# Graph attention over a sparse adjacency: eight largest columns of each row taken with the degree, before the sort, instead of lists made after it

## Chip, cores and metric

One core of one Trainium2 chip. The time is the device time of one execution in microseconds (us); the median of several executions is given, and one further execution was recorded by the hardware profiler.

## The reference

Sixteen graphs of 1024 nodes with 512 features share one 1024 x 1024 adjacency matrix of zeros and ones. One attention layer with 8 heads of 64 is followed by a residual and a layer norm without scale or shift:

```python
q = (x @ Wq + bq).reshape(b, n, H, HD)          # k, v in the same way
scores = jnp.einsum('bqhd,bkhd->bhqk', q, k) / jnp.sqrt(jnp.float32(HD))
scores = scores + (1.0 - adj)[None, None, :, :] * -1000000000.0
attn = jax.nn.softmax(scores, axis=-1)
out = jnp.einsum('bhqk,bkhd->bqhd', attn, v).reshape(b, n, d)
x = _layernorm(x + (out @ Wo + bo), axis=-1)
```

A one at (i, j) has the probability 0.0039 times w[i] w[j], with w falling along the nodes, so that a row has few ones, some rows none and the first rows many. A row without any attends to all nodes alike.

## The kernel before, in words

**Sparse attention by gathers.** The rows are sorted by degree and worked on in eight tiles of 128 sorted rows. A *block* is one neighbour of each of the 128 rows of a tile: the keys and values of those neighbours are gathered from memory (`gather`, L951), VectorE multiplies them with the queries and adds up the heads (`products` L987, `scores` L1000), ScalarE makes the exponentials (L1004) and weighs the values, and VectorE adds the blocks up. Each row's first neighbours are its *own* blocks, `OWN = (2, 1, 2, 3, 4, 5, 5, 7)` for the eight tiles. Only tiles 6 and 7 have rows with more; their further edges are packed into 1 and 5 blocks (`BLOCKS`), where a partition holds any edge of the tile, and TensorE adds these up by a matrix of zeros and ones (`sums`, L1040). This makes 34 blocks a graph (tile 1 needs no block, its rows have one neighbour) and 544 in all.

**Fronts and finish.** A graph's *fronts* are transposes of x (`transpose_x`) and the products q, k, v in pairs of tiles (`pair`, L651), k and v by a seven-product scheme for 2x2 blocks of matrices that needs the weight combinations T1 to T4 (L321 to L326) and the sums of inputs s1 to s4 (`combine`, L615). k and v go to `kv_rows` and q to `q_rows` in memory. A finished tile is multiplied with Wo, normalised and stored in the order of the original rows.

**Order of the work.** The program is written out by hand (`manual_schedule`): a loop over steps `n`, one for a block, from `-LEAD_IN` on. Each step issues block n's work in its stages, then as much TensorE work as its `share` allows: in the lead-in the constants `LEAD_SHARE` and `LISTS_SHARE`, from step 0 on what is left until a goal that the planner sets for the end of each graph. Preparations are generators that advance by one `yield` in each step (`prep`, `preps`). Each engine runs its instructions in the order issued; GpSimd's queue (POOL) issues the indirect gathers, SP's the plain transfers. Four PSUM banks (`fill_psum`) turn round among the products.

**Making the lists, before.** All of this happens once, in front of and within the first graph:

- `ranks` (L370): the adjacency tiles are loaded, ScalarE adds up their rows (L382), the key degree*1024+row is spread over all partitions by TensorE (L392), and VectorE finds each row's rank (L405). (row, degree) is scattered to `order` by rank (L399) and read back in sorted order, `ranked` (L416 to L419), which gives `asked_row`, the original row at each sorted place. From the ranks each column also gets a code, place*2048+column+1, spread by eight more products (L434) into `CODE_OF`.
- `edges(t)` (L467), for each of the eight tiles, from the steps `EDGES_FROM`: gather the tile's adjacency rows in sorted order (L471), multiply with the codes (L477), take the eight largest of each row (L496; tile 7 first in segments of 64, ten rounds), take the code apart into the original row for graph 0 (`key_row0`) and the sorted place for the later graphs (`key_row`) (`decode`, L460), and for tiles 6 and 7 distribute the further edges over the blocks (L528 to L581).
- `checks` (L446): every entry of the adjacency must be 0 or 1; GpSimd clears each tile after it (L454).
- `sort_residual` (L810), at the steps -16 to -4: the rows of x that the last 26 tiles need as a residual are gathered in sorted order and stored to `residual`, from where `load_y` (L815) reads them near the end.

Of the kernel before, what the change touches and what calls it, by code (L numbers as in the profile page):

```python
# [10 lines left out]
F32 = mybir.dt.float32  # L11
BF16 = mybir.dt.bfloat16
I32 = mybir.dt.int32
AF = mybir.ActivationFunctionType
# [19 lines left out]
CODE, ROUND = 2048.0, 12582912.0  # L34
# [7 lines left out]
SORTED_AT = range(-16, -3)  # L42
# [6 lines left out]
LEAD_IN = 34  # L49
SEGMENT = 64  # L50
EDGES_FROM = (-17, -16, -15, -13, -11, -8, -7, -18)
# [4 lines left out]
LEAD_SHARE = 3.45  # L56
LISTS_SHARE = 4.6
# [106 lines left out]
def kernel(  # L164
# [48 lines left out]
    own = [sum(OWN[:t]) for t in range(NT)]  # L213
# [20 lines left out]
    with ExitStack() as main:  # L234
# [16 lines left out]
        SPAN = max(BLOCKS) * P  # L251
# [17 lines left out]
        key_row, key_row0 = (one.tile([P, NB], I32, name=name) for name in ("key_row", "key_row0"))  # L269
        query_row, query_row0 = (one.tile([P, NS], I32, name=name) for name in ("query_row", "query_row0"))  # L270

        absent = one.tile([P, NB - NS], F32, name="absent")
# [6 lines left out]
        asked, ranked = (one.tile([P, NT, 2], F32, name=name) for name in ("asked", "ranked"))  # L279
        key, rank, moved = (one.tile([P, NT], F32, name=name) for name in ("key", "rank", "moved"))  # L280
        rank_row, asked_row = (one.tile([P, NT], I32, name=name) for name in ("rank_row", "asked_row"))
        ADJ, CODE_OF = [], []
# [4 lines left out]
        order = dram.tile([N, 2], F32, name="order")  # L287
# [12 lines left out]
        def loads():  # L300
# [11 lines left out]
            for _ in range(3):  # L312
                yield
# [8 lines left out]
            yield  # L322
            nc.vector.tensor_tensor(T2, B22, T1, op=OP.subtract)
            yield
# [35 lines left out]
        now, plan, rest, urgent, known, waiting = [0], {}, {}, [], [], []  # L360
# [8 lines left out]

        def ranks():  # L370
# [4 lines left out]
            first_order = small.tile([P, 2 * NT], F32, name="order_first", bufs=1)  # L375
            nc.gpsimd.memset(first_order, 0.0)
            nc.gpsimd.dma_start(order.rearrange("(p t) c -> p (t c)", p=P), first_order)
            nc.vector.tensor_copy(asked[:, :, 0], query)
            for _ in range(4):
                yield  # L380
            for t in range(NT):
                nc.scalar.activation(ADJ[t], ADJ[t], AF.Copy, accum_out=asked[:, t, 1:2])  # L382
                if t % 3 == 2:
                    yield

            nc.vector.scalar_tensor_tensor(key, asked[:, :, 1], float(N), query, op0=OP.mult, op1=OP.add)
            keys = work.tile([P, N], F32, tag="kv", name="keys", bufs=5)
# [39 lines left out]
            nc.vector.tensor_tensor(moved, rank, moved, op=OP.add)  # L427
            nc.vector.tensor_scalar(key, query, 1.0, None, op0=OP.add)
            nc.vector.scalar_tensor_tensor(key, moved, CODE, key, op0=OP.mult, op1=OP.add)
# [3 lines left out]
            for t in range(NT):  # L433
                nc.tensor.matmul(pk[t // 4][:, ts(t % 4, P)], keys[:, ts(t, P)], ident, start=True, stop=True)  # L434
# [867 lines left out]
```

## Time and profile before

| | |
|---|---|
| median of 3 runs | 1949.38 us (1948.74 to 1950.09) |
| the profiled execution | 1952.72 us, its span 1951.0 us |
| granted TensorE clock, mean | 0.99 |
| transfers | 551.28 MB, mean 283 GB/s |

The busy tenths of the span's forty equal slices (48.8 us each):

```profile
DVE  2799999899999999899998998989899988999894
ACT  3514978888798888888887888888888888989794
POOL 1664676777677676766767576767767675756684
PEclk9989999999999999999999999999999999999998
DMA  7688888888888887887988788898988888998993
```

PE is TensorE, DVE VectorE, ACT ScalarE, POOL GpSimd. A digit is a tenth of the slice, 9 is 90% or more. In a row of a table of stretches stand the stretch, its length, the busy us of PE, PE's weight loads, DVE, ACT and POOL with their numbers of instructions, TensorE's granted clock, the DMA share and GB/s. In a timeline stand the start, the length, the engine, the line of the program, the operation and its tiles, and in brackets the idle time before it and what ended it. A row of waits names who waited for whom, the sum, how often, and the longest. The instructions that load x the first time and the weights lie in the first 30 us; the first block's product (L998) starts at 153.0 us, and the first graph's blocks end at 296.8 us.

### The profile page before, as it was taken

What the parts mean: (1) busy time and instruction counts of PE and PEld (TensorE: products, weight loads), DVE (VectorE), ACT (ScalarE), POOL (GpSimd) and SP (SyncE); (2) the same over time, 40 slices, a digit from 0 to 9 for tenths busy, and PEclk for the clock granted to TensorE, in tenths of its full rate; (3) what the DMA queues carried; (4) which work ended last, traced back from release to release, by engine and by line L of the source; (5) the groups of instructions that cost most, each with busy time, mean ns of one, the idle gap of its engine ahead of it and who ended that gap; (6) DMA issues with size and microseconds to landing.
All of it is one profiled execution on the core that took longest, in us unless ns stands there. A gap on an engine that the chain in (4) does not pass through costs nothing. (4 is left out here: it accounts for less than half of the span.)

```text
span 1951.0 us, 25391 instructions
## 1 busy us (share of the span) xinstructions
PE 1871.4 (96%) x5275; PEld 903.7 (46%) x5275; DVE 1741.1 (89%) x3604; ACT 1550.1 (79%) x6074; POOL 1295.9 (66%) x1205
## 2 busy tenths in 40 slices
PE   8979999999999999999999999999999999899896
PEld 3434444444545454454544444444544544344443
DVE  2799999899999999899998998989899988999894
ACT  3514978888798888888887888888888888989794
POOL 1664676777677676766767576767767675756684
PEclk9989999999999999999999999999999999999998
DMA  7688888888888887887988788898988888998993
GB/s 264 189 297 286 261 295 270 293 282 298 291 270 311 284 287 268 305 294 254 310 275 307 256 300 278 276 310 258 320 277 293 271 280 296 328 316 266 349 301 137
DMA packets 186050, 551.28 MB, mean 283 GB/s; under 512 B 31295, under 2 KB 31323, under 8 KB 185886
## 3 DMA queue, kind: packets, MB, share of 16 engines
q0 software_dynamic: 120528, 398.76, 62.5%
q1 hardware_dynamic: 62464, 145.30, 20.0%
q10 hardware_dynamic: 2894, 5.52, 0.8%
q14 instruction: 120, 0.98, 0.2%
q8 instruction: 44, 0.72, 0.1%
HBM read 433.86 MB, written 140.30 MB: 294 GB/s over the span
## 5 line engine op out<-in xcount | busy, mean ns | idle before, releaser
L1022 ACT ACTIVATE pv<-kvg,pv 128x64 f32<-128x64 f32 x3544 | 893.1, 339 | 3.2 <-issue 1.9
L977 POOL DMA_INDIRECT kvg<-kv_rows,key_row x544 | 623.6, 1146 | 330.9 <-issue 101.2
L634 PE MATMUL po<-wo,oT 128*128 128x512 f32 x944 | 438.1, 596 | 2.0 <-DVE y L857 1.1
L634 PE MATMUL pq<-wq,xT 128*128 128x512 f32 x904 | 422.5, 598 | 1.7 <-DVE q L664 1.3
L1002 DVE TENSOR_REDUCE s<-qk 128x8 f32<-128x512 f32 x544 | 369.8, 680 | 7.6 <-ACT pv L1012 0.5
L998 DVE TENSOR_TENSOR qk<-qt,kvg 128x512 f32<-128x512 f32 x448 | 306.1, 683 | 10.5 <-DMA kvg<-kv_rows,key_row 10.1
L634 PEld LDWEIGHTS po<-wo,oT 128*128 128x128 f32 x944 | 176.9, 191 | 195.3 <-issue 184.3
L634 PEld LDWEIGHTS pq<-wq,xT 128*128 128x128 f32 x904 | 168.9, 192 | 197.6 <-issue 183.8
L751 PE MATMUL pp<-t,s 128*128 128x512 f32 x504 | 239.2, 597 | 8.4 <-DVE s L620 4.5
L751 PE MATMUL x<-b,xT 128*128 128x512 f32 x504 | 239.7, 598 | 0.0
L1038 DVE TENSOR_TENSOR pv<-pv,pv 128x520 f32<-128x520 f32 x336 | 232.8, 693 | 4.4 <-ACT pv L1022 2.7
L805 POOL DMA_INDIRECT x<-in_x_dram,asked_row x120 | 135.8, 1132 | 89.0 <-PE pxT L605 62.2
L1012 ACT ACTIVATE pv<-s,absent 128x8 f32<-128x8 f32 x448 | 130.4, 293 | 67.0 <-DVE s L1002 48.0
L883 POOL DMA_INDIRECT out_dram<-y,asked_row x128 | 148.5, 1160 | 36.0 <-issue 27.1
L644 ACT ACTIVATE sq_k<-kv 128x128 f32<-128x128 f32 x512 | 150.8, 300 | 20.6 <-DVE kv L774 13.6
L751 PEld LDWEIGHTS pp<-t,s 128*128 128x128 f32 x504 | 95.0, 191 | 121.9 <-issue 114.4
L751 PEld LDWEIGHTS x<-b,xT 128*128 128x128 f32 x504 | 96.1, 193 | 114.1 <-issue 110.0
L805 POOL DMA_INDIRECT y<-in_x_dram,asked_row x102 | 113.4, 1112 | 30.8 <-issue 29.0
L751 PE MATMUL z<-b,s 128*128 128x512 f32 x252 | 121.9, 607 | 11.0 <-DVE kv L779 9.8
L947 POOL DMA_INDIRECT qg<-q_rows,query_row x96 | 105.2, 1096 | 34.0 <-issue 25.4
L751 PE MATMUL pp<-t,xT 128*128 128x512 f32 x252 | 118.5, 593 | 0.4 <-DVE q L664 0.4
L751 PE MATMUL z<-t,s 128*128 128x512 f32 x252 | 118.6, 593 | 0.0
(221 smaller groups left out, 2602.8 us busy)
## 6 DMA issues: line engine op xcount, KB each, us to landing
kv_rows<-kv SPq DMA_DIRECT2D x128, 512.0 KB
q_rows<-q SPq DMA_DIRECT2D x113, 256.0 KB
qt<-q_rows SPq DMA_DIRECT2D x105, 256.0 KB
kvg<-kv_rows,key_row POOLq DMA_INDIRECT x544
residual<-y_sorted SPq DMA_DIRECT2D x26, 256.0 KB
y<-residual SPq DMA_DIRECT2D x26, 256.0 KB
adj<-in_adj_dram POOLq DMA_DIRECT2D x8, 512.0 KB
spill<-oT SPq DMA_DIRECT2D x10, 256.0 KB
```

Source lines behind the costliest of these rows:

```text
L634: nc.tensor.matmul(p, lhs(c), w[:, c, :], start=(c == 0), stop=(c == NPAIR - 1))
L644: nc.scalar.activation(sq, s[:, ts(h, P)], AF.Square, scale=scale, accum_out=sums[:, h:h + 1])
L751: nc.tensor.matmul(R[bank], l[:, ts(c, P)], right[:, c, :], start=(first and c == 0), stop=(c == 1), skip_group_check=True,)
L805: nc.gpsimd.indirect_dma_start(out=y, out_offset=None, in_=x_rows, in_offset=bass.IndirectOffsetOnAxis(ap=asked_row[:, t:t + 1], axis=0), ...
L883: nc.gpsimd.indirect_dma_start(out=out_rows[b, t], out_offset=bass.IndirectOffsetOnAxis(ap=asked_row[:, t:t + 1], axis=0), in_=y, in_offse ...
L947: nc.gpsimd.indirect_dma_start(out=q, out_offset=None, in_=q_rows[b % ROWS], in_offset=bass.IndirectOffsetOnAxis(ap=rows, axis=0))
L977: nc.gpsimd.indirect_dma_start(out=KG[n], out_offset=None, in_=kv_rows[b % ROWS], in_offset=bass.IndirectOffsetOnAxis(ap=keys_of(b)[:, g:g ...
L998: nc.vector.tensor_tensor(QK[n], q, KG[n][:, 0:D], op=OP.mult)
L1002: nc.vector.tensor_reduce(S[n], QK.pop(n).rearrange("p (h d) -> p h d", d=HD), axis=AX.X, op=OP.add)
L1012: nc.scalar.activation(PV[n][:, D:], S.pop(n), AF.Exp, bias=bias)
L1022: nc.scalar.activation(pv[:, ts(h, HD)], v[:, ds(D + h * HD, HD)], AF.Copy, scale=pv[:, D + h:D + h + 1])
L1038: nc.vector.tensor_tensor(PV[b, t], PV[b, t], pv, op=OP.add)
```

## The change

The columns are looked for earlier, in the original order of rows. Right after the adjacency tiles are there (`most`), VectorE multiplies each with the column numbers 1 to 1024 and takes the eight largest of each row (`TOP`). They are scattered together with row and degree, so that `order` and `ranked` have ten numbers a row instead of two. After the sort, the own keys of all eight tiles are made at once from `ranked`. Places are no longer coded: each column's place is stored once to `place_of` in memory, and small indirect gathers (`places`) fetch 128 of them for each own block and each further block, into `key_row`. `edges` stays for tiles 7 and 6 alone (`REST_FROM`) and works with columns, not codes. The code products, `decode`, the clearing of adjacency tiles and the matrix of edges of its own (`of`) go.

T1 to T4 and Wo's load come later in the lead-in, behind most of the column search. `sort_residual` goes; the late tiles of x are stored to `residual` when they have been transposed, and the next load of x comes two steps later there. The lead-in has 39 steps instead of 34, with less TensorE work in its last 13 (`START_SHARE` 2.0 where 4.6 stood in the last 15).

```diff
-SORTED_AT = range(-16, -3)
-LEAD_IN = 34
-EDGES_FROM = (-17, -16, -15, -13, -11, -8, -7, -18)
+LEAD_IN = 39
+FRONT_BY = -14
+TOP = 8
+ADJ_AT = {-36: (0,), -35: (1, 2), -34: (3, 4), -33: (5,), -32: (6, 7)}
+CHECKS_AT = -27
+BIAS_AT = -8
+REST_FROM = {7: -24, 6: -9}
+PLACES_FROM = -22
-LEAD_SHARE = 3.45
-LISTS_SHARE = 4.6
+LEAD_SHARE = 3.3
+START_SHARE = 2.0
...
-            for _ in range(3):
+            for _ in range(5):
                 yield
             load_w(W["o"], wo)
...
+        def most(t, scratch):
+            nc.scalar.activation(ADJ[t], ADJ[t], AF.Copy, accum_out=asked[:, t, 1:2])
+            nc.vector.tensor_tensor(scratch, ADJ[t], place, op=OP.mult)
+            nc.vector.max(out=asked[:, t, 2:], in_=scratch)
...
-            nc.vector.tensor_tensor(moved, rank, moved, op=OP.add)
-            nc.vector.tensor_scalar(key, query, 1.0, None, op0=OP.add)
-            nc.vector.scalar_tensor_tensor(key, moved, CODE, key, op0=OP.mult, op1=OP.add)
-            nc.vector.tensor_copy(keys.rearrange("p (t q) -> p t q", t=NT), key[:, :, None].to_broadcast([P, NT, P]))
-            yield
-            pk = [fill_psum(f"pcodes_{i}") for i in range(2)]
-            for t in range(NT):
-                nc.tensor.matmul(pk[t // 4][:, ts(t % 4, P)], keys[:, ts(t, P)], ident, start=True, stop=True)
...
+            nc.vector.tensor_tensor(place_row, rank, moved, op=OP.add)
+            nc.sync.dma_start(place_of[0:N, :].rearrange("(t p) o -> p (t o)", p=P), place_row)
...
+            nc.vector.tensor_scalar(off, ranked[:, :, 2:3], 0.0, N + 1.0, op0=OP.is_le, op1=OP.mult)
+            nc.vector.tensor_tensor(ranked[:, :, 2:3], ranked[:, :, 2:3], off, op=OP.add)
+            nc.vector.tensor_scalar(ranked[:, :, 2:], ranked[:, :, 2:], -1.0, None, op0=OP.add)
+            yield
+            for tiles, K in ((slice(0, short), SHORT_KEYS), *((slice(t, t + 1), OWN[t]) for t in range(short, NT))):
...
+        def places(columns, per_step):
+            for i, g in enumerate(columns):
+                nc.gpsimd.indirect_dma_start(
+                    out=key_row[:, g:g + 1], out_offset=None, in_=place_of,
+                    in_offset=bass.IndirectOffsetOnAxis(ap=key_row0[:, g:g + 1], axis=0), bounds_check=N, oob_is_err=False,
+                )
...
-            for i in range(2):
-                nc.vector.tensor_tensor(v[:, ts(i, HALF)], v[:, ts(i, HALF)], CODE_OF[i], op=OP.mult)
+            nc.vector.tensor_tensor(v, v, place, op=OP.mult)
...
-            rows, high, missing = kr[:, 0, 0:K], kr[:, 1, 0:K], absent[:, own[t]:own[t] + K]
...
-            decode(rows, high)
...
-                    load_x(n // NT, n % NT)
+                    if b * NT + t >= SPILL[0]:
+                        nc.sync.dma_start(residual[b * NT + t - SPILL[0]], xs)
+                        later(2, lambda: load_x(n // NT, n % NT))
+                    else:
+                        load_x(n // NT, n % NT)
...
-        for t in range(NT):
-            prep.setdefault(EDGES_FROM[t], []).append(edges(t))
-        prep.setdefault(12 - LEAD_IN, []).append(bias_setup())
-        prep.setdefault(-22, []).append(checks())
+        for t, n in REST_FROM.items():
+            prep.setdefault(n, []).append(edges(t))
+        prep.setdefault(BIAS_AT, []).append(bias_setup())
+        prep.setdefault(CHECKS_AT, []).append(checks())
+        prep.setdefault(PLACES_FROM, []).append(places([NS + own[t] + i for t in range(NT) for i in range(OWN[t])], 3))
...
-                    share = LISTS_SHARE if n > -16 else LEAD_SHARE if n > -LEAD_IN else TRANSPOSE * 1.5
+                    share = START_SHARE if n > FRONT_BY else LEAD_SHARE if n > -LEAD_IN else TRANSPOSE * 1.5
...
-                if n in SORTED_AT:
-                    for i in range(2):
-                        sort_residual(2 * (n - SORTED_AT[0]) + i)
```

## The prediction

> **What bounds the kernel now.** I read the page's busy shares first, then the table of stretches (busy us of each engine), then what TensorE waited for in the first 200 us, then the timelines of TensorE and VectorE there.
>
> ```profile
> PE 1871.4 (96%) x5275; PEld 903.7 (46%) x5275; DVE 1741.1 (89%) x3604; ACT 1550.1 (79%) x6074; POOL 1295.9 (66%) x1205
> ```
> ```profile
> 0.00:22.10 22.10, 13.55 (x36) 6.71 (x36) 1.20 (x3) 3.53 (x5) 7.67 (x24) 1.00 0.92 344
> 22.10:48.90 26.80, 26.28 (x73) 12.83 (x74) 13.09 (x23) 14.91 (x40) 0.43 (x1) 0.94 0.53 197
> 75.00:123.90 48.90, 44.36 (x104) 19.41 (x103) 38.06 (x118) 15.53 (x49) 27.94 (x28) 0.93 0.87 298
> 123.90:150.30 26.40, 20.11 (x49) 8.21 (x49) 24.12 (x82) 5.37 (x21) 16.71 (x16) 0.94 0.85 300
> 150.30:297.00 146.70, 140.19 (x409) 68.25 (x408) 137.17 (x306) 108.81 (x456) 88.13 (x81) 1.00 0.83 280
> ```
> ```profile
> PE pxT L605 <- DMA x<-in_x_dram: 6.8, 2, 3.7
> PE pp L751 <- DVE s L620: 4.5, 1, 4.5
> PE z L751 <- DVE kv L779: 4.1, 1, 4.1
> PE pcodes L434 <- DVE keys L430: 2.5, 1, 2.5
> PE pk L723 <- DMA b<-in_L_gnn_Wk_dram: 2.3, 1, 2.3
> PE pp L751 <- DVE s L618: 1.7, 1, 1.7
> ```
> ```profile
> 38.06 1.88 PE L751 MATMUL pp<-t,s 128*128 128x512 f32 x4
> ...
> 112.21 3.75 PE L751 MATMUL pp<-t,s 128*128 128x512 f32 x4 [4.54 <-DVE s L620]
> 115.75 4.74 PE L634 MATMUL pq<-wq,xT 128*128 128x512 f32 x8
> ```
> ```profile
> 28.46 1.22 DVE L325 TENSOR_TENSOR t<-b,b 128x1024 f32<-128x1024 f32 x1
> ...
> 88.04 1.41 DVE L692 TENSOR_TENSOR vsum<-vsum,kv 128x512 f32<-128x512 f32 x2
> ...
> 99.98 1.21 DVE L496 MAX8 kl<-codes 128x8 f32<-128x1024 f32 x1
> ```
>
> TensorE bounds the whole: 1871 of 1951 us. From 297 to 1440 us it is busy 1132.89 of 1143. So only its losses count, and those that the change can touch lie at the front. Batch 0's list of blocks ends at 297 us (L1075's first reduction, at 296.8). Up to there TensorE is busy 268.1 us (the rows above and 23.62 from 48.9 to 75) and idle 28.9. Of that, 6.8 and 2.3 are first loads. The other 19.8 lie behind VectorE, nearly all between 105 and 180 us, where VectorE is busy 24.12 of 26.4 with the lists of all eight tiles. The clock falls with these waits: after the one of 4.54 us a group that takes 1.88 takes 3.75, one of 3.60 takes 4.74; such rows (pp, pq, pxT, z, x between 112 and 140) come to 5.2 us too much.
>
> **What the Trainium skill says.** "TensorE: Matmul & The Clock Gate", What's actually happening: an idle window of some 3.4 us halves the array's clock. The trace agrees: slow groups after 4.54 and 4.14 us, none after 2.48 (pcodes, 2.05 us against 1.95 for pkeys). "GPSIMD Engine Reference", Specifications: GpSimd shares its SBUF interface with VectorE in some modes. The trace fits: an 8-element VectorE operation took 2.29 us at 60.21 while GpSimd cleared two adjacency tiles (L454, 1.86 us). "DMA: Bandwidth & Descriptors", Anatomy of one DMA: about 2 us fixed for each transfer. The trace has 3 us from the last scatter (ends 60.62) to the load behind it (63.56).
>
> **The change, part by part.**
>
> *Lists of tiles 0 to 5 go.* Each has two half products (1.21 from start to start), one MAX8 (1.25) and 13 small operations: tile 0 takes 1.91 (99.98 to 101.89) + 1.21 + 1.31 (106.55 to 107.86) = 4.4 us, six are 26.6 of VectorE between 93 and 182. Tiles 6 and 7 lose decoding, about 2.4 each. Two half products become one of 128x1024, no gain. With them go six adjacency gathers and the second code pass: eight 128x128 products (2.05 on TensorE), its wait of 2.5, and 1 us of VectorE.
>
> *Column search comes.* Eight times a 128x1024 product (1.22) and MAX8 (1.21), each waiting for the other: 2.51 a tile, 20.1 us. It stands behind q of tile 1, which a store held until 22.11, and before T1 to T4, which were made at 25.77 to 30.8. In the changed order of instructions three tiles, the four sums s (1.46), two tiles, `before` (0.2) and a sixth tile stand before T1 and T2: 22.75 + 7.5 + 1.5 + 5.0 + 0.2 + 2.5 + 2.5 = 42.0. TensorE wants T2 at 38.06: it waits 3.9, and at a lower clock loses 2 more. Bounds: 2 (wo's load, now later, leaves the first loads more bandwidth) and 8 (adjacency tiles land late; their landing is not shown).
>
> *Ranks.* Two more tiles, T3, T4, key and keys end at 50.1; TensorE is at the key transposes at 48.9 (42.0 + 1.7 + 3.44 + 1.72) and waits 1.3. The ranks (1.33 each, with what lies between) end at about 66.5 against 57.4. From there to the ranked rows took 11 us (57.4 to 68.47); GpSimd's clearing is gone from it, so I take 9.7: 76.2. VectorE's queue is empty at 71.6 and stands 4.6 us at `asked_row`. Behind it wait q of tile 4, the key rows (3.3 us of small operations, all eight tiles at once) and g. TensorE needs q's PSUM bank at 76.2 and gets it at 77.7: 1.5. Bounds 0 and 6.
>
> *The long list (tile 7).* Starting at 82 instead of 87, with nothing between it but the fronts, VectorE reaches its degree at 113.3. TensorE is at the offset product at 110.4: 2.9 lost. The last key and the mean follow; without the short lists the waits of 4.5, 4.1, 1.7 and 1.7 have nothing to make them. At `pb3`, moved from 76 to about 132, TensorE waits 2.2 for `bvb`, which stands behind tile 6's first passes. Bounds of both together: 1 and 8.
>
> *GpSimd.* 29 gathers of places for the own keys and 6 later come, at 0.96 + 0.30 (the spacing of rows L805): 44 us; 26 residual gathers, six of adjacency rows and eight clearings (0.95) go: 48 us. So the queue is no longer in sum. The first 18 run from 81.5 to 104; x of tile 3 is queued behind them and read at 120. The rest ends at 120.5, before the first kv gather, which cannot go before the mean row lands, about 119.5. Batch 0 uses the original rows, so no block waits for a place. A place gather's landing is not in this trace; with the fixed 2 us above, an estimate, eight in flight keep up with 1.26 each. Cost 0, bounds 0 and 4.
>
> *Residual.* Twenty-six gathers and stores of 256 KB leave the stretch of 80 to 168 us (DMA share 0.87). The stores alone return at the transposes of tiles 102 to 127, on SP, at about 1425 to 1763; the next x gather is two steps later and waits for its buffer's store. A pair of tiles comes every nine steps there, so x is early enough. VectorE bounds the end of this stretch (24.86 of 25 us from 1675). 6.8 MB at some 400 GB/s is 17 us of DMA time over 340 us at a share of 0.87: I take 1 us, bounds -1 and 6.
>
> *Fewer fronts before block 0.* By the planner's constants, 0.66 + 18x3.45 + 15x4.6 = 131.8 us of TensorE work were issued before step 0; now 0.66 + 25x3.3 + 13x2.0 = 109.2. The goal at the end of batch 0 is fixed (224 us), so the share of a step there rises from 3.68 to 4.34. TensorE's work does not change. VectorE's work for 153 to 297 us, 134.5 of 144, loses 11 for lists and gains 8 of fronts, in about 155 us: there is room, but block by block both are close. I take 3 us lost where 6.5 are lost now after 150.3; bounds 0 and 8.
>
> **The sum.** Removable of before: 19.8 idle + 5.2 slow clock + 2.05 pcodes = 27.0. Lost anew: 3.9 + 2 + 1.3 + 1.5 + 2.9 + 2.2 + 3 = 16.8. Gain 10.2, less 1 for the residual: 9.2. The profiled execution took 1952.72 (span 1951.0 and 1.7 around it): 1943.5. The median of the runs, 1949.38, lies 3.3 below it: 1940.2, say **1940**. Likeliest case's own range: 1933 to 1945.4. From the middle on both do the same steps, so what is won by 297 us is kept.
>
> **Rivals.**
> - *More is won.* If the early waits are 2 us (no slow clock) and batch 0 runs clean, the loss is about 7: gain 20 less 1, 1930. For it: idle VectorE before 50 us (14.3 of 48.9 busy) takes over work from where it is full. Against: T2's order is fixed.
> - *No change.* The front's gain is given back in batch 0: 4.34 us of fronts and products with each block, beside VectorE at 93%. Losing 12 there instead of 3 gives 1949. Against: ScalarE 74% and VectorE's sum above.
> - *Slower.* The column search in front of T2 and the ranks: every microsecond by which VectorE is late at T2 or at `asked_row` passes to TensorE, in its order. If the ranked rows come at 88 instead of 76, with T2 at 46, TensorE loses 4 + 10 more: +5, 1954. It decides from about 9 us beyond my times. For it: VectorE would be full from 22 to 70 and its queue has 50 us of work there without a gap. Against: the durations are measured ones.
> - *Doesn't do what it says.* Only tiles 6 and 7 have blocks and their lists remain in the order of instructions; the short lists are really gone. No chance apart.
>
> **How the numbers follow.** Forecast 0.50, more 0.18, no change 0.14, slower 0.18. The range takes in the first, nearly all of the second and third, and of the slower case the mildest: **1929 to 1952**. A measurement of this kernel tells about 0.2% (4 us) from no change. Faster by more, below 1945.5: 0.50 less a little, and 0.18: 0.67. Within: 0.15. Slower: 0.18.
>
> **What would show it.** Right: one TensorE wait of about 4 us for T2 near 38; VectorE's MAX8 of 128x1024 eight times from 23 to 47; `asked_row` near 76 with VectorE idle before it; first block product near 135 instead of 153; L1075's first reduction (now shifted in line) near 287 instead of 296.8; later stretches unchanged. Wrong: TensorE idle again at 100 to 150, places gathers holding back kv gathers, or idle TensorE from 1440 to 1763 beyond the 12 us of now (323 less 310.9).

## The result, and the profile after

The changed kernel took 1972.23 us in the median (1968.62 to 1976.46) against 1949.74 for the kernel before beside it; ratio 1.0106 [1.007, 1.0142]. It is slower by 22 us where 9 us less were forecast. The profiled execution of the changed kernel took 1968.62 us (span 1966.8). Batch 0 below is the first graph; "stretch" is a piece of time in which VectorE stands between its own short instructions.

The busy shares on the page of the changed kernel (the same columns as before):

```profile
PE 1874.8 (95%) x5259; PEld 907.2 (46%) x5259; DVE 1729.9 (88%) x3506; ACT 1549.2 (79%) x6072; POOL 1284.7 (65%) x1201
```

The work is what was foreseen: VectorE has 11 us less, TensorE the same, the span is 15.8 us longer. The first reduction of batch 0 (now L1084) stands at 310.4 us, 13.6 later than before; from there to the last batch's (1944.2) are 1633.8 us against 1631.8. So 13.6 of the 15.8 us between the two profiled executions are lost before 310 us.

What TensorE waited for in the first 200 us of the changed kernel (us in total, times, longest):

```profile
PE z L765 <- DVE kv L793: 8.2, 2, 8.0
...
PE pxT L615 <- DVE w L781: 6.4, 1, 6.4
PE pp L765 <- DVE t L334: 5.7, 1, 5.7
PE pp L765 <- remote: 4.2, 1, 4.2
```

("remote" means that the trace has nothing recorded that ended the wait.)

And its table of stretches:

```profile
75.00:100.00 25.00, 21.59 (x58) 9.56 (x57) 12.81 (x51) 15.43 (x36) 13.11 (x13) 0.99 0.84 159
100.00:125.00 25.00, 12.82 (x24) 5.64 (x25) 11.29 (x39) 1.76 (x9) 19.15 (x19) 0.70 0.15 43
125.00:150.00 25.00, 18.19 (x49) 8.15 (x48) 17.51 (x45) 5.10 (x21) 6.46 (x7) 0.83 0.34 109
```

The hole is between 100 and 125 us: TensorE is busy 12.82 of 25, and the engine for which it waits, VectorE, only 11.29. Neither has too much to do. Two things stand out. First, in the timeline of the changed kernel:

```profile
88.10 1.01 POOL L478 DMA_INDIRECT key_row<-place_of,key_row  x1 [5.29 <-DMA place_of<-place_row]
...
92.49 1.23 DVE L506 TENSOR_TENSOR codes<-codes,place 128x1024 f32<-128x1024 f32 x1 [9.37 <-DMA codes<-in_adj_dram,asked_row]
```

The store of the table of places, 4 KB, was issued at 75.84 and landed about 88. The gather of tile 7's adjacency rows was issued at 78.0 and landed at 92.5; VectorE stood 9.4 us for it. In between the DMA engines are full and move little (the last two numbers are their share and GB/s):

```profile
75.00:80.00 5.00, 4.98 (x18) 2.42 (x18) 2.78 (x20) 4.97 (x11) 1.67 (x2) 1.00 1.14 57
80.00:85.00 5.00, 5.00 (x13) 2.15 (x12) 2.97 (x10) 4.93 (x11) 2.20 (x3) 1.00 0.97 23
```

The store writes 1024 separate elements of four bytes (column t of partition p goes to row t*128 + p): of the 2123 packets from 75 to 90 us, 1150 are of four bytes. By the record these take 7 ns each; the time stands in the pieces of the q, k and v rows that are stored behind them: from 80 to 85 us a piece of 4 KB took 2.3 us in the median, with the 32-byte store below 0.16 to 0.18. Second, from 105 to 132 us VectorE pauses between its own short instructions:

```profile
111.63 0.28 DVE L519 SCALAR_TENSOR_TENSOR codes<-codes,found 128x64 f32<-128x64 f32 x1 [1.78 <-remote]
...
117.22 0.28 DVE L519 SCALAR_TENSOR_TENSOR codes<-codes,found 128x64 f32<-128x64 f32 x1 [2.13 <-remote]
```

What L519 needs, `found` of L518, is made by VectorE itself and was ready 2 us earlier. The stretch falls in the time of GpSimd's 29 gathers of places (L478, 88.1 to 128.6, one every 1.30 us), begins some 13 gathers after the first and ends soon after the last.

### The profile page after: what moved, and what is told of

Same layout as the page of the kernel before. It is cut to its first block, busy times and chain, and to the rows that moved or that the text cites. A ratio compares the mean times of both kernels' runs of the same rounds, so it can differ in the third digit from the quotient of the medians.

```text
span 1966.8 us, 25244 instructions
## 1 busy us (share of the span) xinstructions
PE 1874.8 (95%) x5259; PEld 907.2 (46%) x5259; DVE 1729.9 (88%) x3506; ACT 1549.2 (79%) x6072; POOL 1284.7 (65%) x1201
## 4 chain that ended last, share of the span: by engine, by line
PE 73%; DVE 11%; issue 4%; DMA 4%; ACT 2%; POOL 1%; another core or an unknown queue 1%; SPq 0%; POOLq 0%; DVEq 0%
PE po L648 19%; PE pq L648 15%; PE pp L765 12%; PE z L765 9%; PE x L765 8%; DVE qk L1007 2%; PE poT L1090 2%; PE pxT L615 2%; PE sum L1056 2%; PE sum L1057 2%; DVE s L1011 2%; ACT pv L1031 1%; DVE pv L1047 1%; DMA codes<-in_adj_dram,asked_row 1%; DMA kvg<-kv_rows,key_row 1%
## 5 line engine op out<-in xcount | busy, mean ns | idle before, releaser
L819 POOL DMA_INDIRECT x<-in_x_dram,asked_row x120 | 131.3, 1094 | 71.2 <-PE pxT L615 41.5
```

Of the source, the lines that this page charges most:

```text
L819: nc.gpsimd.indirect_dma_start(out=y, out_offset=None, in_=x_rows, in_offset=bass.IndirectOffsetOnAxis(ap=asked_row[:, t:t + 1], axis=0), ...
```

## The experiments

Theories: **A**, the four-byte store holds the DMA engines, and so tile 7's rows. **B**, the gathers of places slow the other engines. **C**, the slower rival of the prediction: the column search in front of T2 and the ranks. Kernels that are set side by side below ran on one chip, beside the kernel before; there were four chips, numbered here; on which one the changed kernel of the result ran is not recorded. Ratios are to the kernel before on the same chip. The kernels with the 32-byte store, those without gathers of places and the two trains built on them leave something out: graphs 1 to 15 take their keys from other rows, as many and as scattered. They show what a part costs and are no versions to keep.

| kernel | chip | median us | ratio |
|---|---|---|---|
| 32-byte store | 1 | 1956.14 | 1.0026 [1.001, 1.0041] |
| no gathers of places | 1 | 1950.05 | 0.9989 [0.9972, 1.0007] |
| both | 1 | 1940.92 | 0.9946 [0.9927, 0.9965] |
| T2 early | 1 | 1972.28 | 1.0109 [1.0069, 1.015] |
| turned store, places spread | 2 | 1985.25 | 1.0104 [1.0064, 1.0144] |
| train of 512-byte gathers | 2 | 1971.02 | 1.0045 [1.0025, 1.0064] |
| train of valid gathers | 2 | 1970.23 | 1.0041 [1.0025, 1.0058] |
| residual alone, in before | 2 | 1963.75 | 1.0002 [0.9983, 1.002] |
| turned store, paced | 3 | 1933.1 | 0.9963 [0.9949, 0.9977] |
| turned store | 3 | 1927.9 | 0.9941 [0.9925, 0.9957] |
| paced, T2 early | 3 | 1935.54 | 0.9971 [0.9962, 0.9981] |
| changed kernel | 4 | 1967.7 | 1.008 [1.0063, 1.0097] |
| turned store | 4 | 1955.07 | 1.0018 [1.0003, 1.0033] |
| turned store, paced | 4 | 1958.59 | 1.0028 [1.001, 1.0046] |
| no gathers of places | 4 | 1947.55 | 0.9982 [0.997, 0.9994] |
| changed kernel, again | 4 | 1969.33 | 1.0091 [1.0074, 1.0109] |
| turned store, again | 4 | 1956.03 | 1.0028 [1.0013, 1.0043] |

### The store in 32-byte pieces

```diff
-            nc.sync.dma_start(place_of[0:N, :].rearrange("(t p) o -> p (t o)", p=P), place_row)
+            nc.sync.dma_start(place_of[0:N, :].rearrange("(p t) o -> p (t o)", p=P), place_row)
```

> The changed kernel with one edit: the table of places is stored as 128 pieces of 32 bytes (node 8p+t from partition p) instead of 1024 pieces of 4 bytes. So graphs 1 to 15 take their keys from other rows of the table, which are as many and as scattered as before; no instruction is added or removed. Theory A (the 1024 four-byte pieces hold the DMA engines from 76 to 88 us, and so hold up the gather of tile 7's adjacency rows): VectorE's wait for codes_7 at L506 falls from 9.4 us to 3 or less, the multiply starts at 83 to 86 us instead of 92.5, the first place gather starts before 82 us instead of 88.1, batch 0 ends 5 to 9 us sooner than 310.4, and the time is 1963 to 1967 us against 1972. If the store is not what holds the gather (the rival: the adjacency rows are simply slow to come in a stretch with many transfers), L506 still waits 8 us or more and the time stays at 1972 +- 2.

1956.14 us; batch 0 ends at 295.8. The multiply of tile 7's codes in its timeline:

```profile
81.52 1.23 DVE L506 TENSOR_TENSOR codes<-codes,place 128x1024 f32<-128x1024 f32 x1 [1.50 <-DMA codes<-in_adj_dram,asked_row]
```

The wait falls from 9.37 to 1.50 and the rows come 11 us sooner. Some 3 of these lie ahead of the store, whose table was ready at 68.5 instead of 71.1; from the gather's issue (74.9) to its use there are 6.6 us in place of 14.5. A is right, and larger than expected (16 us, not 5 to 9). The slow stretch is still there, only earlier:

```profile
90.00:95.00 5.00, 3.44 (x12) 1.48 (x10) 2.25 (x7) 0.00 (x0) 3.78 (x5) 1.00 0.04 6
95.00:100.00 5.00, 3.83 (x8) 1.36 (x8) 1.74 (x8) 0.00 (x0) 3.78 (x5) 0.66 0.02 0
100.00:105.00 5.00, 0.00 (x0) 0.00 (x0) 1.87 (x7) 0.00 (x0) 2.79 (x3) 0.81 0.02 0
```

VectorE 1.7 to 2.3 of 5 us, ScalarE nothing, the DMA engines empty (0.02), GpSimd alone full (3.78, and 0.30 before each gather).

### No gathers of places

```diff
-            preps.append(places(range(first[t], first[t] + nb), 1))
-        prep.setdefault(PLACES_FROM, []).append(places([NS + own[t] + i for t in range(NT) for i in range(OWN[t])], 3))
```

> The changed kernel without any gather of places: graphs 1 to 15 use the node numbers themselves as rows of the sorted table, so they take their keys from other rows, as many and as scattered. The 42 four-byte-per-partition gathers of the table of places go (13 at 88 to 104 us and 29 at 104 to 129 us); the store of the table stays as it is. Theory B (the gathers of places slow VectorE's short dependent instructions): between 105 and 130 us VectorE is busy 3.5 us or more of each 5 us in place of 1.2 to 2.2, the waits of 0.4 to 2.1 us between its own instructions go, and batch 0 ends 6 to 12 us sooner than 310.4; time 1960 to 1966 us. If the 1.0 to 1.3 us waits are the length of the chain itself (short instructions, each of which needs the one before), nothing changes there: batch 0 ends within 2 us of 310 and the time stays within 2 us of 1972.

The expectation miscounts the gathers: there are 29 for own keys (12 begin before 104 us, 17 after) and six later ones. 1950.05 us, so 22 us and not 6 to 12 come back; batch 0 ends at 292.1. In its table of stretches VectorE is full where it was slow, although tile 7's rows still come late (wait of 8.84 at 91.13):

```profile
105.00:110.00 5.00, 5.00 (x12) 2.12 (x11) 4.59 (x17) 0.00 (x0) 0.41 (x1) 0.90 0.64 203
110.00:115.00 5.00, 5.00 (x13) 2.20 (x12) 4.75 (x12) 0.16 (x1) 0.00 (x0) 1.00 0.00 0
```

B is right too, on this chip: without the gathers the stretch is gone.

### Both

> Both edits together: the table of places stored in 128 pieces of 32 bytes and none of it gathered again; graphs 1 to 15 take their keys from the rows of the node numbers. If A and B are both right and stand one after the other on VectorE's path to tile 7's list, batch 0 ends 12 to 20 us sooner than 310.4 and the time is 1952 to 1960 us, near the kernel before. If the two are one thing (DMA engines filled by four-byte pieces, whichever), the sum is no more than the larger of the two alone. If the rival C holds (the column search in front of T2 and the ranks costs TensorE the time), little is gained: 1966 us or more.

1940.92 us, batch 0 ends at 282.3, tile 7's degree (L538) is made at 114.2, the first block product (L1006) stands at 137.6. The two edits alone give 16.1 and 22.2 us (taken against the kernel with T2 early, which ran on the same chip and takes as long as the changed one); together 31.4, where 12 to 20 were expected. That is far more than the larger of the two alone, so they are two things, not one. The 7 us by which the sum of the single gains exceeds 31.4 mean nothing: the four executions of the kernel with T2 early are uncertain by 8 us. The 31.4 are nearly all of the 32.2 us between forecast (1940) and result (1972.23).

### T1 and T2 two steps earlier

```diff
-            for _ in range(5):
+            for _ in range(4):
                 yield
+            nc.vector.tensor_tensor(T1, B12[0], B11, op=OP.subtract)
+            nc.vector.tensor_tensor(T2, B22, T1, op=OP.subtract)
+            combined.append(True)
+            yield
             load_w(W["o"], wo)
...
-            nc.vector.tensor_tensor(T1, B12[0], B11, op=OP.subtract)
-            nc.vector.tensor_tensor(T2, B22, T1, op=OP.subtract)
-            combined.append(True)
+            yield
```

> The changed kernel with the two subtractions of T1 and T2 two steps earlier, after the third adjacency tile instead of after the sixth; nothing is left out. TensorE's wait for T2 (5.7 us before the first x4 at L765) goes, or falls under 1 us. Rival C (the column search in front of T2 and the ranks is what makes the kernel slower): 4 us or more of the time comes back, 1968 us or less. Theory A+B (VectorE's path through tile 7's list sets the first block): TensorE's first fronts come 5 us sooner but the first block product stays at 174 us give or take 2, TensorE having more empty time between 100 and 130 us instead, and the time falls by 0 to 3 us.

1972.28 us: nothing. (The first block product of the changed kernel stands at 164.0 us, not at 174; here it stands at 162.2.) Two of TensorE's waits in its first 200 us:

```profile
PE z L766 <- DVE g L785: 8.0, 1, 8.0
PE pkeys L409 <- DVE keys L405: 7.1, 1, 7.1
```

The wait for T2 is gone and stands, as 7.1 us, at the transposes of the keys, which are ready only after the whole column search. So this run alone leaves C standing, since the column search is still in front of the ranks. It falls by the run before: the kernel with both edits has the same column search in front of T2 and of the ranks, and is faster than the kernel before.

### What in the gathers is it?

Three kernels on a second chip. The first turns the places with one product and spreads their gathers over the steps:

```diff
-            nc.vector.tensor_tensor(place_row, rank, moved, op=OP.add)
-            nc.sync.dma_start(place_of[0:N, :].rearrange("(t p) o -> p (t o)", p=P), place_row)
-            yield
+            nc.vector.tensor_tensor(moved, rank, moved, op=OP.add)
             yield
+            pl = fill_psum("pplace")
+            nc.tensor.matmul(pl[0:NT, 0:P], moved, ident, start=True, stop=True)
+            yield
             nc.vector.tensor_copy(asked_row, ranked[:, :, 0])
             known.append(True)
+            nc.vector.tensor_copy(place_row, pl[0:NT, 0:P])
+            nc.sync.dma_start(place_of[0:N, :].rearrange("(t p) o -> t (p o)", p=P), place_row)
...
-PLACES_FROM = -22
+PLACES_FROM = -10
```

(and one gather to a step in place of three).

> The changed kernel with both causes mended and nothing left out: the 128x8 tile of places is turned to 8x128 by one product with the identity matrix and stored as 8 pieces of 512 bytes, and the 29 gathers of places of the own keys come one to a step from step -10 on (batch 1 needs them at step 45) in place of three to a step from step -22 on. If A and B are the causes and it is the unbroken train of gathers that slows the engines, batch 0 ends within 4 us of the 282.4 of the kernel without gathers and the time is 1939 to 1945 us. If every gather of places costs about the same wherever it stands (15 us for 29 in the two kernels with the 32-byte store, 0.5 each), the time is 1952 to 1957 us.

1985.25 us, ratio 1.0104: neither expectation holds. The first block product, at 133.2 us, was even earlier than in the kernel with both edits (137.6). Then:

```profile
135.00:140.00 5.00, 5.00 (x13) 2.21 (x12) 3.08 (x5) 0.30 (x1) 3.94 (x4) 1.00 0.46 135
140.00:150.00 10.00, 2.41 (x8) 0.86 (x6) 0.00 (x0) 0.00 (x0) 7.56 (x9) 0.80 0.48 142
```

VectorE and ScalarE do nothing for ten microseconds, TensorE next to nothing, while GpSimd issues one gather after the other: 25 without a pause from 120.5 to 153, places between the gathers of batch 0's keys and queries. "One to a step" doesn't space them: no gather waits for anything, so GpSimd runs ahead through the steps. The train had only been moved. Batch 0 ends at 302.9 us, 20.6 later than in the kernel with both edits on the first chip. But that explains only a small part of the 22 us by which this kernel is slower than the kernel before on its chip: the kernel with the residual tiles alone (below), which is as fast as the kernel before, ends batch 0 there at 300.6. From the first reduction to the last it takes 1640.3 us and this kernel 1657.0; what makes these 17 us is open.

The next two put other trains where the 29 gathers were, in the kernel with both edits: 512 bytes to a partition into tiles that nobody reads; and four bytes with indices that all exist.

```diff
+                nc.gpsimd.indirect_dma_start(
+                    out=y[:, ts(n % 4, P)], out_offset=None, in_=x_rows.rearrange("n (c p) -> (n c) p", p=P),
+                    in_offset=bass.IndirectOffsetOnAxis(ap=key_row0[:, g:g + 1], axis=0), bounds_check=N, oob_is_err=False,
+                )
```

> The kernel with the 32-byte store and no gathers of places (1940.9 us, keys of graphs 1 to 15 from other rows), with 29 gathers put where the 29 own-key gathers of places were, by the same indices, missing ones skipped too, but of 512 bytes to a partition from x into tiles that nobody reads. If the four-byte size is what slows the engines (B1): no stretch with DVE under 3 of 5 us between 88 and 106, 1941 to 1945 us. If the unbroken train of gathers from GpSimd does it whatever their size (B2): the slow stretch is there as with four bytes, and the time is 1952 to 1960 us.

> As the run before, but the 29 gathers are of four bytes from the table of places into a scratch tile and by indices that all exist (no row is skipped). If skipped rows are the cause (B3): no slow stretch, 1941 to 1945 us. If B1 or B2: slow stretch as with the gathers of places, 1952 to 1958 us.

1.0045 and 1.0041, the same as each other and near the 1.0026 of the gathers of places with the 32-byte store on the first chip. In their tables VectorE is slow too, 1.10 and 2.58 from 95 to 100 us (512 bytes first):

```profile
95.00:100.00 5.00, 0.57 (x5) 0.33 (x3) 1.10 (x3) 0.00 (x0) 3.93 (x4) 0.89 0.15 43
```
```profile
95.00:100.00 5.00, 1.96 (x10) 1.35 (x9) 2.58 (x7) 0.00 (x0) 3.82 (x4) 0.87 0.01 0
```

So neither the size of the element nor the skipped rows make the stretch; a long train of GpSimd's gathers is common to all these kernels. A price in us is not read here, since the kernel without any train was not run on this chip, whose kernel before took 1963.19.

### The residual tiles alone

```diff
-                    load_x(n // NT, n % NT)
+                    if b * NT + t >= SPILL[0]:
+                        nc.sync.dma_start(residual[b * NT + t - SPILL[0]], xs)
+                        later(2, lambda: load_x(n // NT, n % NT))
+                    else:
+                        load_x(n // NT, n % NT)
...
-                if n in SORTED_AT:
-                    for i in range(2):
-                        sort_residual(2 * (n - SORTED_AT[0]) + i)
```

> The kernel before with one part of the change alone: no sorted copies of the ten last x tiles by 26 gathers of GpSimd before block 0; the last tiles are stored from their transposes, with the next x load two steps later. Nothing is left out. If the y_sorted gathers cost time in the kernel before as the places do in the changed one (a train of gathers), 1938 to 1945 us; the prediction had them beside other work and their place in the late steps at +1 us (-1 to 6): 1948 to 1956 us.

1.0002 [0.9983, 1.002]: this part (26 tiles, not ten) neither wins nor loses.

### The store mended, and the gathers paced

The paced kernel has the turned store, and VectorE copies each column of indices in the step in which its gather is due, so that GpSimd has to wait for it:

```diff
+                nc.vector.tensor_copy(key_at[:, g:g + 1], key_row0[:, g:g + 1])
                 nc.gpsimd.indirect_dma_start(
                     out=key_row[:, g:g + 1], out_offset=None, in_=place_of,
-                    in_offset=bass.IndirectOffsetOnAxis(ap=key_row0[:, g:g + 1], axis=0), bounds_check=N, oob_is_err=False,
+                    in_offset=bass.IndirectOffsetOnAxis(ap=key_at[:, g:g + 1], axis=0), bounds_check=N, oob_is_err=False,
                 )
```

> The changed kernel, nothing left out, with the 8x512-byte store of the places and with the same 35 gathers of places, but paced: each takes its index from a one-column copy that VectorE makes at that step, so that GpSimd cannot run ahead; three in two steps from step -21 to -10, none from step -9 to 2 (where the gathers of block keys begin), then one in three steps, and those of the deep lists from step 30. If it is the unbroken train that costs (theory B as the last runs left it), no stretch with VectorE under 3.5 of 5 us between 80 and 135 us, batch 0 ends at 280 to 290 us and the ratio to the kernel before is 0.993 to 0.998 (before, on the same chip, 1.0; the kernel without any gathers had 0.9946). If each gather of places costs its 0.5 us wherever it stands, the ratio is 1.002 or more.

> The changed kernel with the store of the places turned to 8 pieces of 512 bytes and nothing else: the gathers of places stand in one train as in the changed kernel. Theory A alone mended: the gather of tile 7's rows lands before 85 us in place of 92.5, VectorE is slow (under 2.5 of 5 us) from about 90 to 106 us, and the ratio is that of the 32-byte store, 1.0026, give or take 0.003. Were the store harmless, 1.0106 as the changed kernel.

> The paced kernel and T1, T2 two steps earlier. In the changed kernel the earlier T2 gave nothing (1972.28 against 1972.23), because TensorE then waited at the transposes of the keys instead. Theory: here too the path to the first block is VectorE's, and the ratio is that of the paced kernel within 0.002. Rival: with A and B out of the way the wait for T2 (3.9 to 5.7 us) lies on the path that sets the end, and the ratio falls by 0.002 to 0.003 more.

On this third chip all three are faster than the kernel before: paced 0.9963, with T2 early 0.9971 (as the theory had it), and the best is the one that was to be slow, the turned store with the train as it was: 0.9941 [0.9925, 0.9957]. Its train is unbroken from 80.6 to 123.5 us, and VectorE is not slowed by it (4.5 to 4.8 of each 5 us from 85 to 115). Batch 0 ends at 281.9 us, with all 35 gathers, as it does at 282.3 without any on the first chip. Here the train costs nothing that can be seen. Two theories were set against each other: the four-byte store starts the stretch (K), or the stretch belongs to the chip (P). Against K speak already the 32-byte store on the first chip and the turned store on the second, which both had it.

### The same kernels on a fourth chip

> The changed kernel once more, on the same chip as the next three. Its ratio to before was 1.0106. If the slow stretch of all engines belongs to the chip (theory P), it can be missing here; then VectorE is busy over 3.5 of each 5 us from 95 to 125 us and the ratio is about 0.998 to 1.002, the loss by the four-byte store alone. If it belongs to the kernel (theory K), the stretch is there on every chip and the ratio is 1.008 to 1.013.

> The turned store with the train of gathers once more (0.9941 on another chip, without a slow stretch). Theory K (the four-byte store is what starts the slow stretch): no slow stretch here either, 0.993 to 0.996, while the changed kernel beside it has one. Theory P: on a chip where the changed kernel has the slow stretch, this one has it too, from about 90 to 106 us, and its ratio is 1.000 to 1.005.

> The turned store with paced gathers (0.9963 beside 0.9941 for the train). Theory K: again about 0.002 above the train. Theory P on a chip with slow trains: 0.994 to 0.998, below the train by 0.003 or more.

> The changed kernel without any gather of places (keys of graphs 1 to 15 by node number, from other rows), four-byte store kept; 0.9989 beside 1.0106 before. Theory P on a chip without slow trains: no more than 0.003 below the changed kernel. Theory K, or P on a chip with slow trains: again 0.010 or more below it.

The changed kernel has its slow stretch here (1.008), and so has the turned store (1.0018). One kernel, two chips; first the third chip, then the fourth:

```profile
95.00:100.00 5.00, 5.00 (x16) 2.37 (x15) 4.63 (x16) 2.22 (x10) 3.78 (x5) 1.00 0.16 53
100.00:105.00 5.00, 5.00 (x13) 2.22 (x12) 4.72 (x13) 0.00 (x0) 4.04 (x4) 1.00 0.02 2
```
```profile
95.00:100.00 5.00, 2.37 (x8) 1.07 (x8) 2.10 (x8) 0.00 (x0) 3.86 (x4) 1.00 0.02 0
100.00:105.00 5.00, 0.00 (x0) 0.00 (x0) 0.92 (x4) 0.00 (x0) 2.99 (x3) 0.86 0.02 0
```

GpSimd does nearly the same in both, VectorE 9.35 or 3.02 of 10 us. That is theory P: the stretch belongs to the chip, as far as one chip without it, seen in three kernels at one time, can show that. The paced kernel had it as well on the fourth chip, not around 95 us, where its gathers are spaced, but from 129 to 140, in a train of 19 gathers without a pause (113.0 to 137.7 us): six of places, then the codes of tile 6, rows of x and the queries and keys of batch 0's blocks. Third chip, then fourth:

```profile
130.00:135.00 5.00, 4.32 (x12) 1.63 (x10) 4.75 (x7) 2.13 (x9) 3.78 (x5) 1.00 0.90 305
135.00:140.00 5.00, 2.71 (x7) 1.28 (x8) 4.90 (x9) 0.30 (x1) 3.18 (x3) 1.00 1.01 401
```
```profile
130.00:135.00 5.00, 3.37 (x10) 1.37 (x9) 0.00 (x0) 0.59 (x1) 3.91 (x4) 1.00 0.81 256
135.00:140.00 5.00, 2.38 (x6) 0.68 (x4) 0.69 (x1) 1.44 (x9) 2.04 (x3) 1.00 0.83 245
```

The pacing thus saved nothing that the block gathers didn't take back: 1.0028 beside 1.0018, where P had expected a gain of 0.003 or more. Without gathers of places the ratio is 0.9982.

> The changed kernel on one more chip. Theory P (the slow stretch belongs to the chip): either the stretch is there in this run and in the next, and the ratios are 1.008 to 1.011 and 1.000 to 1.004; or it is in neither, and the ratios are 0.998 to 1.003 (only the four-byte store lost) and 0.992 to 0.996. The stretch in one of the two kernels alone would speak against P.

> The turned store with the train of gathers on the same chip as the run before. Theory P: as said there, the stretch (VectorE under 2.5 of 5 us between 90 and 106 us) is here if and only if it is in the changed kernel between 105 and 132 us; in both cases this kernel is 0.004 to 0.009 of the time faster than the changed one, which is the price of the four-byte store.

Both ran on the fourth chip again, not on a further one: 1.0091 and 1.0028, both with the stretch. They repeat the pair, no more. The changed kernel was not seen on a chip without the stretch.

### What the stretch is made of

The trace also keeps when each semaphore was raised. Set beside the ends of the VectorE instructions that raise it, in the turned store (us):

```
third chip                               fourth chip
ends    raised                           ends    raised
93.30   93.31                            97.10   98.81
93.69   93.70                            99.12   99.51
94.01   94.02                            99.89  101.61
94.40   94.41                           104.72  105.11
```

A semaphore is the counter by which one instruction tells the next that it is done. On the fourth chip the instruction is done and its semaphore is raised 0.4 to 1.7 us late; VectorE starts 0.02 us after each. The list leaves out instructions whose raising is not in the trace. The timeline of VectorE there:

```profile
98.83 0.28 DVE L522 SCALAR_TENSOR_TENSOR codes<-codes,found 128x64 f32<-128x64 f32 x1 [1.73 <-remote]
99.53 0.23 DVE L523 MAX8 found<-codes 128x8 f32<-128x64 f32 x1 [0.42 <-DVE codes L522]
...
101.63 0.28 DVE L522 SCALAR_TENSOR_TENSOR codes<-codes,found 128x64 f32<-128x64 f32 x1 [1.75 <-remote]
102.33 0.23 DVE L523 MAX8 found<-codes 128x8 f32<-128x64 f32 x1 [0.42 <-issue]
...
104.44 0.28 DVE L522 SCALAR_TENSOR_TENSOR codes<-codes,found 128x64 f32<-128x64 f32 x1 [1.75 <-remote]
```

These starts lie 0.70 or 2.1 us apart: a grid of 0.70 us. Other engines are held too. In the 32-byte-store kernel on the first chip TensorE, VectorE, ScalarE and SyncE all go on within 0.04 us of each other at 106.0. SyncE had waited for VectorE's q, done at 104.73, TensorE for VectorE too, and ScalarE for a product of TensorE that had ended at 91.3, 14.7 us earlier. So in the stretch it is the semaphore of a finished instruction that comes late. What delays it, and why one chip has none of it, is open.

A second sign goes with the chips. On the third one the trace of the turned store has every raising of VectorE's semaphore in the whole execution, none more than 0.013 us late, and the two paced kernels have them all too. In every other trace, that of the kernel before included, a quarter is missing (2394 to 2540 recorded of some 3300). And the kernel before has the stretch as well, at the end of twelve gathers in a row (1165.2 to 1181.0 us): ScalarE's instruction there had ended at 1178.48.

```profile
1180.40 0.40 ACT L644 ACTIVATE sq_q<-qt,lone 128x128 f32<-128x128 f32 x1 [1.92 <-ACT sq_q L644]
```

So the stretch is no property of the change; the change adds a place where it occurs, on the path to the first block. Whether the missing records and the late semaphores have one cause is not shown. That the recording makes the delay is unlikely, since the medians follow the profiles although only one execution of each kernel is recorded (1955.07 on the fourth chip and 1927.9 on the third, spans 1953.5 and 1924.1).

"SBUF — State Buffer" in the Trainium skill, Who interferes with whom, names one way in which GpSimd and VectorE hold each other up: a VectorE instruction that reads two operands from SBUF contends with a GpSimd instruction that reads SBUF. That doesn't fit as the cause here: ScalarE is held just as long, and what is late is the semaphore of an instruction already done.

## Why the prediction was wrong

**The two steps that failed.** (1) "GpSimd", the term "Cost 0, bounds 0 and 4" for the gathers of places: measured 15.2 us (32-byte store with and without them, first chip), 22.2 us (four-byte store, first chip) and 20.2 us (fourth chip: 1967.7 less 1947.55). The working asked only whether the queue has time for them (44 us come, 48 go) and whether a block waits for a place. Both answers held: the gathers are issued every 1.30 us and no block of batch 0 uses one. What it didn't ask is what else stands while a train of gathers runs. On the third chip, where nothing does, the zero would have held. (2) The store of the table of places had no term at all. Measured: 9.1 us (without gathers), 16.1 us (with them), 12.6 and 13.3 us on the fourth chip. The step "The long list (tile 7)" let VectorE begin at 82 us; in the trace the rows, asked for at 78.0, landed at 92.5, after the 1024 pieces of four bytes and what was held up behind them, and with the 32-byte store VectorE began at 81.5. The prediction cited the fixed 2 us of a transfer from "DMA: Bandwidth & Descriptors" in the Trainium skill. The same page's Specifications ask for 512 bytes or more to a transfer for full rate, and say that below this the DMA does a read-modify-write. The trace agrees in direction for the pieces of four bytes (4 KB in 12 us), but 128 pieces of 32 bytes, also below 512, held up nothing; whether a read-modify-write is what took the time is not shown.

**The rest held, in part by luck.** With both taken away the kernel takes 1940.92 us on the first chip, or 0.9946 of 1949.74, which is 1939.2; forecast 1940. Tile 7's degree: 113.3 forecast, 114.2 there. First block product: 135, and 137.6. Batch 0's end: 287, and 282.3, so the 3 us for fewer fronts before block 0 were too many. That the total still comes out within 1 us is luck: the 4.7 us won there are offset by what follows (below). And of the 19.8 idle us that the prediction put down to VectorE, the trace of before gives VectorE 15.2; the others stand under "issue" (3.3) and ScalarE (1.2). In the turned store on the third chip, with the gathers left in: 112.6, 135.2 and 281.9.

**T2 and the ranks.** `asked_row` was forecast at 76.2 and stood at 77.0. The wait for T2 was 5.67, not 3.9, and the lower clock behind it took 2.9 us, not 2 (on the fourth chip the same kernel waited 3.78). The changed kernel's timeline of TensorE:

```profile
42.70 3.75 PE L765 MATMUL pp<-t,s 128*128 128x512 f32 x4 [5.67 <-DVE t L334]
46.24 4.21 PE L648 MATMUL pq<-wq,xT 128*128 128x512 f32 x7
```

The wait at the key transposes, 1.3, wasn't there. The sum of the three terms, 7.2 forecast, was 8.6. With T2 early it is 9.3 (a wait of 7.1 and 2.2 at a lower clock): it belongs to the column search as a whole, and moving T2 only moves the place where it is paid. That is also why the slower rival, built on this wait, named the right sign for the wrong reason.

**Residual and tail.** Forecast +1; alone in the kernel before the edit gave 1.0002. From batch 0's end to the last the changed kernel takes 2.0 us longer than before, the kernel with both edits 4.6 (1636.4 against 1631.8): within the bounds of -1 to 6, above the value taken. Profiles of one kernel on one chip differ there by some 4 us (1632.8 and 1636.6 for the changed kernel on the fourth), so more can't be said of this term.

**The version to keep** is the turned store, eight pieces of 512 bytes: faster than the changed kernel on the fourth chip, where both ran twice (by 0.6 and 0.7%), faster than the kernel before on the third chip (0.9941), not on the fourth (1.0018 [1.0003, 1.0033], 1.0028 [1.0013, 1.0043]).

## What to carry to other kernels

Price every new DMA by its pieces and not by its bytes alone: a small table written element by element can hold up a large transfer behind it, and one small product that turns it first is cheap (TensorE waited 0.7 us for it here). Whether the number of the pieces or their size did it was not told apart. A queue that has time for its work isn't yet free: look at what else slows while it runs without a pause, and remember that instructions spread over the program's steps are not spread in time unless something makes them wait. Before a verdict of a per cent or less is carried on, run the two kernels on more than one chip.

## What was not expected of the hardware

- 1024 four-byte writes to HBM in one transfer of 4 KB: landed 12 us after issue, DMA share 0.97 to 1.14 at 23 to 57 GB/s meanwhile. The recorded time stands in the stores behind it (2.3 us for a piece of 4 KB from 80 to 85 us), and a 512 KB gather issued 2 us later landed after 14 us in place of some 6. As 8 pieces of 512 bytes or 128 of 32 it is not noticed.
- Late in a train of back-to-back gathers of GpSimd (1.30 us each, of four bytes or 512), VectorE's semaphores were raised 0.4 to 2.4 us late on a grid of 0.70 us. In eight traces it began 11 to 14 gathers after the start of the train, in a ninth after 23. Once one of TensorE's reached ScalarE 14.7 us late. This was seen on three of the four numbered chips, and in the kernel before too. On the other chip, in 43 us of such a train, they were 0.01 us late as always. Not every train had it: in the 32-byte-store kernel the second one, 108.9 to 123.5 us, left VectorE at 4.75 of 5 us.
- On the chip without late semaphores all raisings are in the traces of three kernels; on the others a quarter of VectorE's is missing, whatever the kernel.
